# Layer 0 of a convolution and attention network: reciprocals of the softmax sums straight from PSUM, and the logits' bound on ScalarE and GpSimd

## The chip, the cores and the metric

The kernel runs on one core of a Trainium2 chip. The metric is the device time of one execution in microseconds (us). The core's engines work side by side, each through its own instructions in order: TensorE (PE in the profile, PEld for its weight loads), VectorE (DVE), ScalarE (ACT), GpSimd (POOL) and the queue of SyncE (SP), which issues the DMAs. SBUF is the memory that the engines work in, with 128 partitions; PSUM holds what TensorE writes.

## What is computed

Four layers follow each other on an input of 4 images of 128 channels and 64 x 64 pixels. Only layer 0 is concerned here. For one image, with q and v maps of 128 x 4096 and two maps w and b of 4096 values, it computes

```python
norm = jnp.sqrt(jnp.sum(q * q, axis=0))
k = q / jnp.clip(norm, 0.0001)[None, :]
logits = jnp.einsum('cn,cm->nm', k, q)
mean = jnp.mean(logits, axis=0, keepdims=True)
sparse = jax.nn.relu(logits - mean * w[None, :] + b[None, :])
mask = (sparse != 0.0).astype(logits.dtype)
attn = jax.nn.softmax(logits * sparse * SOFTMAX_SCALE, axis=0)
attn = jnp.clip(attn * mask, 1e-08)
out = jnp.einsum('cn,nm->cm', v, attn)
```

and then a 3 x 3 convolution of `out`, a leaky ReLU and the sum with the input. Here w and b come from small networks of q, with a leaky ReLU between two 1 x 1 convolutions.

## The kernel before

Layers 0 and 1 run one after the other for each image, with parts of layer 2 of the image before beside them; layer 3 comes last. Layer 0 is `layer0`. It cuts the 4096 columns m of an image into 8 chunks c of `NB` = 512, and the 4096 rows n into 16 pairs of 128. An item i is one chunk with one pair; there are 128 items in an image, and i = 16 c + m. In what follows "item m" is the place in the chunk. An item's tiles are 128 x 2 x 512.

The logits aren't divided by the softmax's sum before the product with v. `weights` computes max(logits + ncut, 0) x logits, where `ncut` is the negated threshold; `shifted` subtracts `bound`, an upper bound of the logits' products in a column, and takes the exponential; `sums` adds up the exponentials with TensorE, in four groups of 32 equal rows of one PSUM bank (`zs`). The clipping at 1e-8 of the quotient is a maximum with the sum times 1e-8 (`floored`, with `floor` in PSUM), and the division comes after the product with v, in `image`, as a factor `scale`. `masked` multiplies with the mask, on VectorE for even items and on GpSimd for odd ones, where ScalarE's Sign has made the mask first. `bound` is max(norm + ncut, 0) x norm for each column; the steps `top` and `top_b` of `thresholds` compute it.

The order of instructions is written out by hand and kept: `pinned` wraps the engines so that the program's order is each engine's order. The loop of `layer0` runs over the items. In item i VectorE does `weights` for i, `above` for i + 1 (logits + ncut) and `floored` for i - 18 (`LAG` is 18); TensorE does `logits` for i + 2, `product` for i - 19 and, every other item, `sums`; GpSimd does the subtraction of `shifted`, and every other item a masked product; ScalarE does the exponential, every other item a Sign, and in images 1 to 3 what `beside` calls: two exponentials over a row of layer 2 of the image before (`junk` in the profile), each with a read of its sum, and a load of `gp` every 16 items. The tile `t` has 21 buffers, so `above` waits for the product of an item 20 before it; the pairs of logits have two PSUM buffers, so `logits` waits for `weights` two items before it.

The small work of a chunk goes through `queue`, a list of runs of steps. In each item at most two steps that aren't marked `on_pe` are taken, until one that is marked comes up, and then that one. Where a run ends without a marked step, the first steps of the next run follow if there is room. These runs matter:

- `scales(c)`: its step `a` copies `zs` at item 0 of the next chunk; the others are put ahead of everything at item 1. `d` makes `floor` with a matmul and the sums as columns with four small ones (`zt_ps`); `f` takes the reciprocals of 128 x 4 (`rzt`); `g` spreads them to 128 x 512 with four matmuls (`rz_ps`); `h` copies this to `scale`.
- `thresholds(c + 1)`: put at the end of the queue at item 1. A load of `q` and `own` (the norms), four matmuls into `th_ps` with the steps `hidden`, `mean`, `times`, `cut` that use each, then `top` on GpSimd and `top_b` on VectorE.
- `convolved`: put at the end at item 3, just after `image`. Six steps with the nine taps, `leaky` on ScalarE, `add` on GpSimd with the store of x1.

The banks of PSUM are all in use: the pairs of logits have four, and `misc` (for `zt_ps`, `rz_ps`, `th_ps`, `conv_ps`, `v_ps`), `zs`, `fl` and `acc` one each. A step that takes a new `misc` tile waits until the old one has been read.

The lines L111 in the profile are those of a helper that records every pinned instruction, so groups are told apart by their tiles.

Of the kernel before, what the change touches and what calls it, by code (L numbers as in the profile page):

```python
# [8 lines left out]
F32 = mybir.dt.float32  # L9
BF16 = mybir.dt.bfloat16  # L10
AF = mybir.ActivationFunctionType
ALU = mybir.AluOpType
# [4 lines left out]
P = 128  # L17
IMG = 64
L = IMG * IMG
PADW = IMG + 2  # L20
NB = 512
# [8 lines left out]
class Queue:  # L30
# [21 lines left out]
    def on_pe(self):  # L52

        if not self.run and self.runs:
            self.run = self.runs.pop(0)
        return bool(self.run) and getattr(self.run[0], "pe", False)
# [59 lines left out]
class Net:  # L116
# [160 lines left out]
    def weights0(self):  # L277
        nc, pool = self.nc, self.later
        self.load_all(pool, ["lin_b"])
        self.load_rows(pool, ["lw2_b", "bw2_b"])  # L280

        M = self.ins["lw1_wT"].shape[1]
        self.w1_T = pool.tile([P, 2 * M], F32, name="w1_T", tag="w1_T")
        self.w1_b = pool.tile([2 * M, 1], F32, name="w1_b", tag="w1_b")
        self.w2 = pool.tile([2 * M, 2], F32, name="w2", tag="w2")
        nc.vector.memset(self.w2, 0.0)
        for i, n in enumerate(("lw", "bw")):
            r = slice(i * M, (i + 1) * M)
            nc.sync.dma_start(out=self.w1_T[:, r], in_=self.ins[f"{n}1_wT"])
            nc.sync.dma_start(out=self.w1_b[r, :], in_=self.ins[f"{n}1_b"])  # L290
            nc.sync.dma_start(out=self.w2[r, i : i + 1], in_=self.ins[f"{n}2_wT"])
        self.lw2_rep = self.replicated(pool, "lw2_rep", self.w2[:, 0:1])
        self.bw2_rep = self.replicated(pool, "bw2_rep", self.w2[:, 1:2])

        self.floor_c = pool.tile([P, P], F32, name="floor_c", tag="floor_c")
        nc.vector.memset(self.floor_c, 1e-8 / 32)
        self.quarter = pool.tile([P, 1], F32, name="quarter", tag="quarter")
        nc.vector.memset(self.quarter, 1.0 / 32)

    def weights12(self):  # L300
        nc, pool = self.nc, self.later
# [31 lines left out]
    def layer0(self, b):  # L333


        nc = self.nc
        pe, dve, act, pool, sp = self.pinned()
# [4 lines left out]
        with self.pool("l0", 1) as big, self.pool("l0t", 2) as tmp, self.pool("l0a", LAG + 3) as ap, \  # L342
# [6 lines left out]
            def misc(name, rows=P):  # L349
                return ps1.tile([rows, NB], F32, name=name, tag="misc")  # L350

            def row(name, bufs=2, rows=P):
                return tmp.tile([rows, NB], F32, name=name, tag=name, bufs=bufs)
# [8 lines left out]
            for c in range(0 if b else NCH):  # L362
                s = bass.ts(c, NB)
# [10 lines left out]
                own = row("own")  # L374
# [11 lines left out]
                for i in range(4):  # L386
                    nc.tensor.matmul(
                        inv_ps[:, bass.ts(i, P)], inv[:, i : i + 1].to_broadcast([P, P]), self.ident,
                        start=True, stop=True,
# [12 lines left out]
            held = {}  # L402
# [18 lines left out]
            qs, ncut, bound = {}, {}, {}  # L421

            def thresholds(c):


                s = bass.ts(c, NB)

                def load():
                    qs[c] = held["q"] = row("q")
                    sp.dma_start(out=qs[c], in_=self.q0[:, s])  # L430
                    held["own"] = row("own")
                    sp.dma_start(out=held["own"], in_=self.norms[:, s].to_broadcast([P, NB]))

                def into(rows, lhsT, key):
                    def go():
                        held["ps"] = misc("th_ps", rows)
                        pe.matmul(held["ps"], lhsT, held[key], start=True, stop=True)
                    return on_pe(go)

                def hidden():  # L440
                    held["h"] = row("h", 1, 64)
                    act.activation(held["h"], held["ps"], AF.Prelu, bias=self.w1_b, alpha=0.2)

                def mean():
                    held["m"] = row("m", 1)
                    act.copy(held["m"], held["ps"])

                def times():
                    dve.scalar_tensor_tensor(held["m"], held["ps"], self.lw2_b, held["m"], ALU.add, ALU.mult)

                def cut():
                    ncut[c] = row("ncut")
                    dve.scalar_tensor_tensor(ncut[c], held["ps"], self.bw2_b, held["m"], ALU.add, ALU.subtract)

                def top():
                    bound[c] = row("bound")
                    pool.tensor_tensor(bound[c], held["own"], ncut[c], ALU.add)

                def top_b():
                    dve.scalar_tensor_tensor(bound[c], bound[c], 0.0, held["own"], ALU.max, ALU.mult)  # L460

                return [
                    load, into(64, self.w1_T, "q"), hidden, into(P, kbar_rep, "q"), mean,
                    into(P, self.lw2_rep, "h"), times, into(P, self.bw2_rep, "h"), cut, top, top_b,
                ]

            def both(t):
# [2 lines left out]
            lg, t, e, zs, acc, floor, scale = {}, {}, {}, {}, {}, {}, {}  # L470
# [58 lines left out]
            def scales(c):  # L529

                def a():
                    held["z"] = row("z", 1)
                    act.copy(held["z"], zs.pop(c))

                def d():
                    floor[c] = ps1.tile([P, NB], F32, name="fl", tag="fl")
                    pe.matmul(floor[c], self.floor_c, held["z"], start=True, stop=True)
                    held["zt"] = misc("zt_ps")
                    for i in range(NB // P):
                        pe.matmul(  # L540
                            held["zt"][:, i : i + 1], held["z"][:, bass.ts(i, P)], self.quarter,
                            start=True, stop=True,
                        )

                def f():
                    held["rz"] = tmp.tile([P, NB // P], F32, name="rzt", tag="rzt")
                    dve.reciprocal(held["rz"], held["zt"][:, 0 : NB // P])

                def g():
                    held["zt"] = misc("rz_ps")  # L550
                    for i in range(NB // P):
                        pe.matmul(
                            held["zt"][:, bass.ts(i, P)], held["rz"][:, i : i + 1].to_broadcast([P, P]),
                            self.ident, start=True, stop=True,
                        )

                def h():
                    scale[c] = row("scale")
                    act.copy(scale[c], held["zt"])

                return [a, on_pe(d), f, on_pe(g), h]

            def image(c):
                dve.tensor_tensor(
                    ypad[:, 1 + c * ROWS : 1 + (c + 1) * ROWS, 1 : 1 + IMG],
                    acc.pop(c).rearrange("p (a b) -> p a b", b=IMG),
                    scale.pop(c).rearrange("p (a b) -> p a b", b=IMG), ALU.mult,
                )

            def convolved(c):  # L570
# [27 lines left out]

            beside = self.row_weights(b - 1, big, tmp) if b else lambda i: None
            queue.add(thresholds(0))  # L600
            if b:
                queue.step()
# [12 lines left out]
            for i in range(S + LAG + 2):  # L615
                c, m = divmod(i, U)
# [13 lines left out]
                if i in due:  # L630
                    d = due.pop(i)
                    image(d)
                    if d:
                        queue.add(convolved(d - 1))
                    if d == NCH - 1:
                        queue.add(convolved(d))
# [4 lines left out]
                if 0 < i <= S + 1:  # L641
                    if i <= S:
                        masked(i - 1)
                    if i % 2 == 0:
                        sums(i - 2)
                    if i % U == 0:
                        run = scales(i // U - 1)
                        run[0]()
                    elif i % U == 1 and i > U:
                        queue.first(run[1:])  # L650
                if i < S and m == 1 and c + 1 < NCH:
                    (queue.add if c else queue.first)(thresholds(c + 1))
# [1348 lines left out]
```

## Time and profile before

| what | value |
|---|---|
| median of three runs | 10654.12 us (10645.72 to 10660.42) |
| the profiled execution | 10664.21 us, of it a span of 10662.4 us from first to last instruction |
| mean granted TensorE clock | 0.896 |
| busy over the span: PE, DVE, ACT, POOL | 80%, 86%, 59%, 76% |
| `weights` of the first to the last item, image 0 | 65.1 to 689.1 us, 624.0 us |
| the same, image 1 | 1724.0 to 2362.4 us, 638.4 us |
| the same, image 2 | 3420.1 to 4057.8 us, 637.7 us |
| the same, image 3 | 5113.6 to 5751.9 us, 638.2 us |

Times are counted from the first instruction of the span. In a group of the profile the columns are line, engine, operation, tiles (written<-read), shapes and count, then busy time, the mean of one in ns, and the idle time just before it with what ended that. In a timeline they are start, duration (both us), engine, line, operation, tiles, shapes and count, with the idle time before it in square brackets. Durations of neighbours on one engine overlap by some 0.08 us, so a step's share of an engine is the distance between starts. The settled chunks of an image, 2 to 6, repeat themselves to within a few hundredths of a us, item by item.

### The profile page before, as it was taken

The numbers are of one execution on the slowest core, as the hardware profiler recorded it, in microseconds if no ns is written. First come the engines' busy times: TensorE is split into PE (matmuls) and PEld (weight loads), VectorE is DVE, ScalarE is ACT, GpSimd is POOL, SyncE is SP. The second block draws the span as 40 slices with busy tenths as digits, with TensorE's granted clock in tenths as the row PEclk, the third lists the DMA queues.
The fourth block names the chain that finished last, engine by engine and source line by source line (L and its number), as shares of the span: only waits on it lengthen the run. The fifth ranks groups of instructions, "written<-read, shape, count | busy, mean of one in ns | idle before, by whom it ended". The sixth has DMA issues, their size and how long they took to land. (4 is left out here: it accounts for less than half of the span.)

```text
span 10662.4 us, 91085 instructions
## 1 busy us (share of the span) xinstructions
PE 8514.6 (80%) x28080; PEld 3044.8 (29%) x28080; DVE 9216.5 (86%) x6390; ACT 6331.1 (59%) x9504; POOL 8117.2 (76%) x3542
## 2 busy tenths in 40 slices
PE   8996667997787997787898778877777777777775
PEld 3331212332223333223333222322222222222221
DVE  7869998886998885999886899449999999999996
ACT  3324445665665664666564666456666666666764
POOL 6748886765887774888674888339999999988986
PEclk9997778998998998999999899889898888888886
DMA  1008773006886003888100888248888888888886
GB/s 37 11 20 196 190 190 94 17 12 159 207 201 163 12 18 88 199 209 205 41 15 22 208 201 204 61 107 205 201 204 201 204 198 207 211 224 222 222 222 178
DMA packets 509431, 1543.30 MB, mean 145 GB/s; under 512 B 84208, under 2 KB 92016, under 8 KB 508944
## 3 DMA queue, kind: packets, MB, share of 16 engines
q1 hardware_dynamic: 508944, 1537.49, 58.1%
q8 instruction: 223, 3.65, 0.2%
q14 instruction: 264, 2.16, 0.1%
HBM read 1342.06 MB, written 132.24 MB: 138 GB/s over the span
## 5 line engine op out<-in xcount | busy, mean ns | idle before, releaser
L111 POOL TENSOR_TENSOR p<-h,c_rep 128x1024 f32<-128x1024 f32 x2048 | 4808.1, 2358 | 831.1 <-DVE h L111 769.9
L111 DVE TENSOR_TENSOR_SCAN h<-da,carry,db 128x1024 f32<-128x1024 f32 x1536 | 3603.6, 2346 | 198.0 <-ACT da L111 20.8
L111 PE MATMUL db<-parts,sel 96*128 96x512 bf16 x4096 | 1401.0, 428 | 1489.7 <-DVE h L111 1469.0
L111 DVE TENSOR_TENSOR db<-b_rep,db 128x1024 f32<-128x1024 f32 x1536 | 1854.5, 1207 | 195.7 <-DMA b_rep<-bc 128.6
L111 ACT ACTIVATE da<-row,A 128x1024 f32<-128x1024 f32 x1536 | 1761.0, 1147 | 321.5 <-DMA row<-d 318.2
L111 POOL TENSOR_TENSOR e<-e,bound 128x1024 f32<-128x1024 f32 x512 | 1240.7, 2425 | 572.6 <-DVE e L111 572.3
L111 POOL TENSOR_TENSOR x<-row,b_rep 128x1024 f32<-128x1024 f32 x512 | 1209.2, 2362 | 155.2 <-DMA row<-d 155.1
L111 PE MATMUL total<-p,gather 128*32 128x512 f32 x8192 | 1251.2, 730 | 10.4 <-POOL p L111 10.2
L111 DVE TENSOR_TENSOR_SCAN h<-db,carry,x 128x1024 f32<-128x1024 f32 x512 | 1194.8, 2334 | 72.5 <-ACT db L111 39.7
L111 ACT ACTIVATE db<-db,A 128x1024 f32<-128x1024 f32 x512 | 555.4, 1085 | 1149.9 <-PE db L111 1095.8
L111 PEld LDWEIGHTS <-sel 96*128 96x128 bf16 x4096 | 309.5, 101 | 3048.3 <-DVE h L111 2091.0
L111 ACT ACTIVATE e<-e 128x1024 f32<-128x1024 f32 x512 | 540.9, 1057 | 1054.3 <-POOL e L111 1054.3
L111 PE MATMUL lg<-q,k 128*128 128x512 f32 x2048 | 1022.8, 623 | 107.4 <-DVE e L111 99.0
L111 PE MATMUL acc<-t,vT 128*128 128x512 f32 x2048 | 956.1, 593 | 6.4 <-DVE t L111 3.3
L111 PE MATMUL acc<-e,values 128*128 128x512 f32 x1536 | 848.2, 643 | 92.0 <-ACT e L111 68.0
L111 DVE TENSOR_TENSOR t<-lg,ncut 128x1024 f32<-128x1024 f32 x512 | 624.6, 1220 | 286.0 <-PE acc L111 262.4
L111 ACT ACT_TABLE_LOAD x617 | 791.6, 1283 | 38.9 <-DMA r<-y 17.6
L111 ACT COPY carry<-h 128x1 f32<-128x1 f32 x2048 | 374.0, 185 | 487.5 <-DVE h L111 483.0
L111 ACT ACTIVATE e<-gq,below,fcol 128x512 f32<-128x512 f32 x768 | 610.1, 805 | 86.7 <-PE acc L111 86.5
L111 POOL TENSOR_TENSOR t<-t,e 128x1024 f32<-128x1024 f32 x256 | 609.9, 2383 | 45.4 <-ACT t L111 45.4
L111 ACT ACTIVATE junk<-gp,ntop,fcol 128x512 f32<-128x512 f32 x768 | 619.5, 807 | 26.8 <-DMA gp<-g 14.1
L111 DVE SCALAR_TENSOR_TENSOR e<-t,lg 128x1024 f32<-128x1024 f32 x512 | 618.9, 1209 | 1.2
(233 smaller groups left out, 9982.4 us busy)
## 6 DMA issues: line engine op xcount, KB each, us to landing
row<-d SPq DMA_DIRECT2D x2048, 512.0 KB
parts<-split SPq DMA_DIRECT2D x960, 64.0 KB
b_rep<-bc SPq DMA_DIRECT2D x96, 512.0 KB
c_rep<-bc SPq DMA_DIRECT2D x96, 512.0 KB
d<-delta SPq DMA_DIRECT2D x80, 384.0 KB
r<-y SPq DMA_DIRECT2D x48, 512.0 KB
xq<-in_x SPq DMA_DIRECT2D x72, 256.0 KB
res<-x SPq DMA_DIRECT2D x32, 512.0 KB
```

Of the source, the lines that this page charges most:

```text
L111: return self.tc.keep_in_program_order(method(*args, **kwargs))
```

## The change

Two parts, both in layer 0. In `scales` the four small matmuls for `zt_ps`, the reciprocals of 128 x 4, the four matmuls for `rz_ps` and the copy go. VectorE takes the reciprocal of `floor` in PSUM into `scale` in four pieces of 128 x 128, as four steps of the queue; `image` multiplies by 1e-8 as well, with another form of instruction. The constant `quarter` goes. In `thresholds`, `top_b` becomes a Relu on ScalarE, and a new step `top_c` multiplies by the norms on GpSimd.

```diff
-        self.quarter = pool.tile([P, 1], F32, name="quarter", tag="quarter")
-        nc.vector.memset(self.quarter, 1.0 / 32)
...
                 def top_b():
-                    dve.scalar_tensor_tensor(bound[c], bound[c], 0.0, held["own"], ALU.max, ALU.mult)
+                    act.activation(bound[c], bound[c], AF.Relu)
+
+                def top_c():
+                    pool.tensor_tensor(bound[c], bound[c], held["own"], ALU.mult)
...
                 def d():
                     floor[c] = ps1.tile([P, NB], F32, name="fl", tag="fl")
                     pe.matmul(floor[c], self.floor_c, held["z"], start=True, stop=True)
-                    held["zt"] = misc("zt_ps")
-                    for i in range(NB // P):
-                        pe.matmul(
-                            held["zt"][:, i : i + 1], held["z"][:, bass.ts(i, P)], self.quarter,
-                            start=True, stop=True,
-                        )
-
-                def f():
-                    held["rz"] = tmp.tile([P, NB // P], F32, name="rzt", tag="rzt")
-                    dve.reciprocal(held["rz"], held["zt"][:, 0 : NB // P])
-
-                def g():
-                    held["zt"] = misc("rz_ps")
-                    for i in range(NB // P):
-                        pe.matmul(
-                            held["zt"][:, bass.ts(i, P)], held["rz"][:, i : i + 1].to_broadcast([P, P]),
-                            self.ident, start=True, stop=True,
-                        )
-
-                def h():
-                    scale[c] = row("scale")
-                    act.copy(scale[c], held["zt"])
-
-                return [a, on_pe(d), f, on_pe(g), h]
+
+                def f(j):
+                    def go():
+                        if j == 0:
+                            scale[c] = row("scale")
+                        s = bass.ts(j, P)
+                        dve.reciprocal(scale[c][:, s], floor[c][:, s])
+                    return go
+
+                return [a, on_pe(d), *[f(j) for j in range(NB // P)]]
...
-                dve.tensor_tensor(
+                dve.scalar_tensor_tensor(
                     ypad[:, 1 + c * ROWS : 1 + (c + 1) * ROWS, 1 : 1 + IMG],
-                    acc.pop(c).rearrange("p (a b) -> p a b", b=IMG),
-                    scale.pop(c).rearrange("p (a b) -> p a b", b=IMG), ALU.mult,
+                    acc.pop(c).rearrange("p (a b) -> p a b", b=IMG), 1e-8,
+                    scale.pop(c).rearrange("p (a b) -> p a b", b=IMG), ALU.mult, ALU.mult,
                 )
```

## The prediction, as put on record

> **What bounds it now.** I read the slices of the page first (second view). They show four stretches with no DMA to speak of and TensorE at 9 tenths: layer 0 of the four images. The view of windows over those stretches comes next:
>
> ```profile
> 65.00:690.00 625.00, 590.77 (x1780) 231.23 (x1779) 549.93 (x473) 211.31 (x224) 465.87 (x202) 0.98 0.05 14
> 1724.00:2363.00 639.00, 589.15 (x1779) 230.18 (x1778) 558.20 (x469) 424.82 (x727) 465.27 (x202) 0.99 0.05 15
> ```
>
> Its columns are the stretch, its length, then busy time of PE, PEld, DVE, ACT and POOL, the granted clock, DMA. PE is busy 92 to 95%, DVE 87 to 88%, POOL 73%: no engine is the bound alone. ACT does twice as much in images 1 to 3 (424.8 against 211.3 us), because two `junk` pairs of `row_weights` follow each exponential there. The groups by line then give prices:
>
> ```profile
> L111 DVE SCALAR_TENSOR_TENSOR bound<-bound,own 128x512 f32<-128x512 f32 x32 | 75.6, 2364 | 6.1 <-POOL bound L111 6.1
> L111 DVE TENSOR_TENSOR t<-lg,ncut 128x1024 f32<-128x1024 f32 x512 | 624.6, 1220 | 286.0 <-PE acc L111 262.4 <-PE lg L111 23.5
> L111 POOL TENSOR_TENSOR e<-e,bound 128x1024 f32<-128x1024 f32 x512 | 1240.7, 2425 | 572.6 <-DVE e L111 572.3
> L111 DVE RECIPROCAL rzt<-zt_ps 128x4 f32<-128x4 f32 x32 | 5.5, 172 | 12.8 <-PE zt_ps L111 12.8
> ```
>
> DVE waits for PE (`above` for the product that frees its tile, 262 us), POOL for DVE (572 us). So place decides, not totals, and the timeline of one settled chunk (image 1, chunk 4) is the view that carries the rest. DVE at items 2 to 4:
>
> ```profile
> 2053.61 0.17 DVE L111 RECIPROCAL rzt<-zt_ps 128x4 f32<-128x4 f32 x1
> 2053.71 1.19 DVE L111 SCALAR_TENSOR_TENSOR e<-t,lg 128x1024 f32<-128x1024 f32 x1
> 2055.73 1.23 DVE L111 TENSOR_TENSOR t<-lg,ncut 128x1024 f32<-128x1024 f32 x1 [0.83 <-PE acc L111]
> ...
> 2061.25 1.23 DVE L111 TENSOR_TENSOR t<-lg,ncut 128x1024 f32<-128x1024 f32 x1 [0.30 <-PE acc L111]
> ...
> 2084.73 2.75 DVE L111 SCALAR_TENSOR_TENSOR bound<-bound,own 128x512 f32<-128x512 f32 x1
> ```
>
> An item begins at `e<-t,lg`. Item 2 runs from 2050.22 to 2053.71 (3.49 us) and is full of DVE work: no idle time is printed in it. PE in the same items:
>
> ```profile
> 2051.20 0.95 PE L111 MATMUL zt_ps<-quarter,z 128*128 128x1 f32 x8
> 2056.61 1.16 PE L111 MATMUL rz_ps<-ident,rzt 128*128 128x128 f32 x8
> 2061.88 1.07 PE L111 MATMUL th_ps<-q,w_T 128*64 128x512 f32 x2 [0.67 <-ACT scale L111]
> 2088.76 1.95 PE L111 MATMUL lg<-q,k 128*128 128x512 f32 x4 [0.83 <-DVE e L111]
> ```
>
> Up to the next start the two groups take 0.81 and 1.00 us, and PE waits 0.67 us for ScalarE's copy of `scale`.
>
> **What the Trainium skill says.** *SBUF — State Buffer*, section "SBUF: two separate sides": a VectorE operation with two SBUF inputs and a GpSimd operation exclude each other for a whole instruction. The trace agrees: `bound` takes 0.69 us at its shortest, and 2.75 when it comes 0.17 us after a GpSimd product. *VectorE: DVE Perf Modes*, "First, the fixed hardware budget": Reciprocal is an iterative divide with a repeat count of 8. The trace has no long one; see below. *ScalarE: Activation LUTs*, "Table sets: the hidden batching unit": relu is in every set. So no table load; no run here shows it, though Sign, Prelu and Exp alternate in this chunk without one. *TensorE: Matmul & The Clock Gate*, "Architectural detail": ScalarE's and VectorE's queues are strictly in order. It agrees: `y<-conv_ps` starts at 2118.04, when the junk pairs ahead of it are over.
>
> **Reciprocals, per chunk.** Removed: 16 small matmuls (1.81 us of PE), the 0.67 us wait, one 0.10 us DVE step, a 0.57 us copy on ScalarE. Added: four reciprocals of 128x128 from PSUM. After idle time one column takes 164 ns (`z`), four 183 (`rzt`, its longest), eight 203 (`split`): 5.6 ns a column. An estimate from this: 164 + 127 x 5.6 = 0.88 us, and as the next instruction starts some 0.08 us before an end, 0.80 us each. Bounds: one column a cycle (1.13 us / 1024 = 1.1 ns) gives 0.22; the page's eight cycles a column give 8 x 1.1 x 128 = 1.15 us. Eight columns at 203 speak against both ends. `image` becomes a form that costs 745 instead of 688 ns (as `ncut`, one PSUM input): +0.06. The scale is read some 16 items later, so it isn't late.
>
> Where it lands: the old queue ran d | f, g | h, and threshold steps. The new one runs d at item 1, two reciprocals at item 2, two at item 3, and no PE step follows there. DVE's item 2 has no slack: 3.49 becomes 3.39 + 1.60 = 4.99. Item 3 gets 1.60 + 0.06 and loses its 0.83 wait, since PE is now ahead. Item 4 loses 0.40 (3.79 to 3.39: the 0.30 and a slower start), item 5 about 0.5 of its 1.89 wait. So 3.20 + 0.06 - 0.10 is added, 0.83 + 0.40 + 0.50 comes back: **+1.4 us a chunk**. The PE time saved is in these recovered waits and nowhere else, because DVE ends last at items 2 and 3. With 0.22 us each it is about 0; with 1.15 it is +2.9.
>
> All later steps of the queue move one item on: the loads of `q` and `own` (still issued with the step ahead of the first threshold matmul; the 16 items hold the whole queue), the threshold matmuls, nine taps, `leaky`, `add`. SP's store of x1 moves with `add`, and the next `gp` load stands behind it; ScalarE waits up to 0.5 us a chunk for `gp` now, and I count nothing for it.
>
> **The bound, per chunk with a threshold behind it.** DVE loses its 2.75 us instruction. Items 8 and 9 took 6.55 + 4.74 = 11.29 us; items 12 and 13, with taps and without it, 3.92 + 6.29 = 10.21: -1.08. Added: a Relu of about 0.6 us (ACT's exponential of 1024 columns takes 1.06, half of it and its start) and a POOL product of 1.28 (as `bound<-own,ncut`). POOL's product waits for the Relu, and the Relu stands behind ACT's exponential of its item and the two junk pairs; behind the product in POOL's queue stands the next subtraction `e<-e,bound`. This is a wait that was not there:
>
> ```profile
> 2091.18 1.06 ACT L111 ACTIVATE e<-e 128x1024 f32<-128x1024 f32 x1 [3.74 <-POOL e L111]
> 2093.88 1.04 ACT L111 ACTIVATE t<-t 128x1024 f32<-128x1024 f32 x1
> 2093.43 2.37 POOL L111 TENSOR_TENSOR e<-e,bound 128x1024 f32<-128x1024 f32 x1 [2.29 <-DVE e L111]
> 2118.78 1.28 POOL L111 TENSOR_TENSOR y<-y,xq 128x512 f32<-128x512 f32 x1 [1.15 <-ACT y L111]
> 2122.41 1.06 ACT L111 ACTIVATE e<-e 128x1024 f32<-128x1024 f32 x1 [3.71 <-POOL e L111]
> ```
>
> Walked on with these durations: the Relu takes the place at 2093.88, POOL's product runs 2094.5 to 2095.8, the subtraction starts at 2095.8 in place of 2093.43, 2.4 late. POOL's masked product ends at 2100.5, DVE's masked product (ready at 2099.89) goes between, the next subtraction ends at 2104.0 (before 2100.44), its exponential and two junk pairs at 2106.8, Sign at 2107.8, the masked product that waits for Sign at 2110.2, the next subtraction at 2112.5; DVE's masked product, which ran at 2110.53, stands at the lock until then: 2.0 us lost on DVE. A precedent lies at item 15: `add`'s wait for `leaky` behind junk makes it 7.38 us, against 6.28 in image 0, 1.10 more. I take 2.5: 2.0 and some of a second such catch. Bounds: 0 (the lag is absorbed, POOL being busy 73%) and 4. Net +1.4 in images 1 to 3. In image 0 the Relu follows at once and delays POOL 0.6 us, which I take as hidden: -1.08.
>
> **The sum.** Images 1 to 3: 3 x (8 x 1.4 + 7 x 1.42) = 63.4. Image 0: 8 x 1.4 - 7 x 1.08 = 3.6. Together +67 us on the profiled span of 10662.4 (10664.2 with what lies around it), +0.63%; the profiled run is 10 above the median of 10654.1. On the median: **10722**. Only one memset in the start-up goes; layers 1 to 3 keep their instructions.
>
> **Rivals.** (1) *TensorE bounds layer 0, and its relief is the gain.* For it: 92 to 95% busy. Place: items 1 to 4; price: 2.48 us a chunk less 0.84 for four reciprocals of 0.22; it decides if these are that short and POOL's lag is absorbed. Then 32 x -1.64 - 28 x 1.08 = -83: 10571. Against it: eight columns at 203 ns, and DVE without slack at item 2. (2) *The lag is absorbed*, reciprocals as forecast: 32 x 1.4 - 28 x 1.08 = +15: 10669, no change. For it: POOL's 27% of idle time; against: item 15. (3) *Reciprocals at eight cycles a column*: 32 x 2.9 + 21 x 1.42 - 7.6 = +115: 10769. For it: the skill's repeat count; against: the eight-column row. That the change doesn't do what it says I leave out: the floor is the sum times 1e-8, and `image` multiplies by 1e-8.
>
> **How the numbers follow.** Forecast 0.62, rival 1 0.09, rival 2 0.12, rival 3 0.17. About 0.2% (21 us) is what a measurement can tell from no change. Faster 0.09, same 0.12, slower 0.79. The reciprocal's bounds shift the forecast by -45 to +48, the stall's by -53 to +32; taken together some -70 to +55. Cut at rival 2's side and at rival 3's: 10655 to 10775.
>
> **What would show it.** Right: reciprocals near 0.88 us; items 2 and 3 longer by 1.5 and 0.8; PE waits there for DVE's `e`; a new POOL wait for ACT's `bound` of 1 us or more in images 1 to 3, none to speak of in image 0; image 0 nearly unchanged, the others some 20 us longer. Wrong: reciprocals under 0.5 us, or layer 0 shorter in all images with DVE still waiting for PE at items 2 to 5; or the time outside layer 0 changing.

## The result, and the profile after

| what | before | after |
|---|---|---|
| median of six runs each | 10652.09 us (10645.72 to 10660.42) | 10719.32 us (10711.84 to 10733.21) |
| ratio after / before, 95% interval | | 1.0064 [1.0051, 1.0077] |
| the profiled execution, its span | 10664.21, 10662.4 us | 10718.85, 10717.1 us |
| layer 0, image 0 (first to last `weights`) | 624.0 us | 629.3 us |
| layer 0, images 1, 2, 3 | 638.4, 637.7, 638.2 us | 655.2, 655.2, 655.3 us |

The kernel became 67 us slower by the medians and 54.6 by the two profiled executions, since the one of before lay 12 us above its median. Layer 0 grew by 56.7 us; the stretches before, between and after changed by -2 us in total. So in this pair the whole loss is in layer 0: +5.3 us in image 0, +17 in each of the others.

The view of windows of the changed kernel, over layer 0 of images 0 and 1 (columns as before: stretch, length, busy PE, PEld, DVE, ACT, POOL, clock, DMA):

```profile
65.00:694.00 629.00, 575.95 (x1666) 216.80 (x1664) 570.55 (x486) 211.37 (x223) 471.66 (x208) 0.99 0.05 14
1731.00:2386.00 655.00, 587.30 (x1665) 219.83 (x1664) 585.30 (x482) 422.81 (x726) 486.92 (x208) 0.97 0.05 15
```

PE has some 114 matmuls less and is busy 90 to 92% instead of 92 to 95%; what it was relieved of did not shorten the stage. DVE went from 558.2 to 585.3 us in image 1. The groups by line of the changed kernel say with what:

```profile
L111 DVE TENSOR_TENSOR t<-lg,ncut 128x1024 f32<-128x1024 f32 x512 | 624.2, 1219 | 232.8 <-PE acc L111 201.8 <-PE lg L111 29.1
L111 POOL TENSOR_TENSOR t<-t,e 128x1024 f32<-128x1024 f32 x256 | 607.1, 2372 | 120.2 <-ACT t L111 120.2
L111 DVE SCALAR_TENSOR_TENSOR t<-t,e 128x1024 f32<-128x1024 f32 x256 | 520.0, 2031 | 26.3 <-ACT e L111 25.7
L111 DVE RECIPROCAL scale<-fl 128x128 f32<-128x128 f32 x128 | 112.0, 918 | 8.8 <-PE fl L111 8.8
L111 POOL TENSOR_TENSOR bound<-bound,own 128x512 f32<-128x512 f32 x32 | 41.8, 1306 | 78.0 <-ACT bound L111 74.7 <-DVE t L111 3.3
```

Of these, the two masked products have to be set beside the same groups of the kernel before, which were not shown yet:

```profile
L111 POOL TENSOR_TENSOR t<-t,e 128x1024 f32<-128x1024 f32 x256 | 609.9, 2383 | 45.4 <-ACT t L111 45.4
L111 DVE SCALAR_TENSOR_TENSOR t<-t,e 128x1024 f32<-128x1024 f32 x256 | 428.0, 1672 | 18.8 <-ACT e L111 18.5
```

Four readings. The reciprocals cost 112 us in all. DVE's idle time before `above` fell from 286 to 233 us (its wait for PE's product from 262 to 202), so part of this is taken from idle time. DVE's masked product is the same instruction on the same data, and yet its mean rose from 1672 to 2031 ns, 92 us in all. That is waiting, which the profile counts as busy: this instruction reads two tiles in SBUF, and it and a GpSimd instruction exclude each other, as the prediction cites. Below this exclusion is called the lock. And POOL has two new idle times: 74.7 us for ACT's Relu (`bound`) and 75 more for ACT's Sign (120.2 against 45.4).

DVE at items 2 to 4 of the chunk that the prediction used (image 1, chunk 4), timeline of the changed kernel:

```profile
2065.31 1.21 DVE L111 SCALAR_TENSOR_TENSOR e<-t,lg 128x1024 f32<-128x1024 f32 x1
...
2069.42 1.76 DVE L111 RECIPROCAL scale<-fl 128x128 f32<-128x128 f32 x2
2071.10 1.16 DVE L111 SCALAR_TENSOR_TENSOR e<-t,lg 128x1024 f32<-128x1024 f32 x1
...
2075.04 2.19 DVE L111 SCALAR_TENSOR_TENSOR t<-t,e 128x1024 f32<-128x1024 f32 x1
2077.15 1.75 DVE L111 RECIPROCAL scale<-fl 128x128 f32<-128x128 f32 x2
2078.83 1.16 DVE L111 SCALAR_TENSOR_TENSOR e<-t,lg 128x1024 f32<-128x1024 f32 x1
```

Item 2 is now 5.79 us (2065.31 to 2071.10), item 3 7.73. That is +2.30 and +1.71, more than the reciprocals alone bring (+1.58 and +0.73, run e1 below). The rest is a wait of 0.63 us for `floor` in item 2, whose matmul waits for a late copy of the sums on ScalarE, and in item 3 the masked product, which takes 2.19 us here and 1.22 before and in e1. TensorE stands behind it, in its own timeline there:

```profile
2075.27 1.96 PE L111 MATMUL acc<-t,vT 128*128 128x512 f32 x4 [0.68 <-DVE ypad L111]
2080.04 3.43 PE L111 MATMUL lg<-q,k 128*128 128x512 f32 x4 [2.82 <-DVE e L111]
```

Before, DVE waited there for PE (0.83 us, shown in the prediction); now PE waits 2.82 us for DVE's `e`. The other part lies at items 10 to 13, where the Relu is. ACT in the timeline:

```profile
2109.09 1.06 ACT L111 ACTIVATE e<-e 128x1024 f32<-128x1024 f32 x1 [3.09 <-POOL e L111]
2110.06 0.80 ACT L111 ACTIVATE junk<-gp,ntop,fcol 128x512 f32<-128x512 f32 x1
...
2110.98 0.81 ACT L111 ACTIVATE junk<-gp,ntop,fcol 128x512 f32<-128x512 f32 x1
...
2111.80 0.62 ACT L111 ACTIVATE bound<-bound 128x512 f32<-128x512 f32 x1
```

and POOL in the same items:

```profile
2112.49 1.28 POOL L111 TENSOR_TENSOR bound<-bound,own 128x512 f32<-128x512 f32 x1 [3.42 <-ACT bound L111]
2113.72 2.37 POOL L111 TENSOR_TENSOR e<-e,bound 128x1024 f32<-128x1024 f32 x1
...
2125.57 2.39 POOL L111 TENSOR_TENSOR t<-t,e 128x1024 f32<-128x1024 f32 x1 [1.52 <-ACT t L111]
2127.91 2.35 POOL L111 TENSOR_TENSOR e<-e,bound 128x1024 f32<-128x1024 f32 x1
```

and DVE's masked product at item 13, in the kernel before and in the changed one:

```profile
2110.53 1.22 DVE L111 SCALAR_TENSOR_TENSOR t<-t,e 128x1024 f32<-128x1024 f32 x1
...
2127.97 3.37 DVE L111 SCALAR_TENSOR_TENSOR t<-t,e 128x1024 f32<-128x1024 f32 x1
```

It reads as the prediction walked it: the Relu behind the exponential and two junk pairs, POOL idle for 3.42 us, its queue late, then a second wait of 1.52 us for Sign, and at the end DVE's masked product, which starts 0.06 us after POOL's subtraction (2127.91), waits out the whole of it and takes 3.37 us instead of the 1.22 that it needs when nothing is in its way.

To see what a chunk gained and lost, I added up, from the trace, what the masked products took over 1.22 us each ("lock"), VectorE's idle time, nearly all of it for `acc`, and its own instruction on `bound`. Each is the mean of chunks 3 to 6, called a settled chunk below. (Chunk 2, which the text ahead of the prediction counts among the settled ones, takes 79.2 us in images 1 to 3 before, not 82.5.) All in us:

| kernel, images | chunk | lock | DVE idle | DVE on `bound` |
|---|---|---|---|---|
| before, image 0 | 80.38 | 1.70 | 10.01 | 2.23 |
| before, images 1 to 3 | 82.49 | 2.62 | 10.75 | 2.75 |
| after, image 0 | 81.09 | 4.37 | 7.16 | 0 |
| after, images 1 to 3 | 84.59 | 6.82 | 8.23 | 0 |

In images 1 to 3, four reciprocals at a spacing of 0.84 add 3.36, `rzt` goes (-0.10), `bound` goes (-2.67 as a spacing), the lock adds 4.20, and 2.52 of idle time is used up: +2.27, where the chunk grew by 2.10. In image 0 it is 3.36 - 0.10 - 2.16 + 2.67 - 2.85 = +0.92, for +0.71.

### The profile page after: what moved, and what is told of

The parts are those of the page before. It is cut to its first block, busy times and chain, and to the rows that moved or that the text cites. A ratio compares the mean times of both kernels' runs of the same rounds, so it can differ in the third digit from the quotient of the medians.

```text
span 10717.1 us, 90072 instructions
## 1 busy us (share of the span) xinstructions
PE 8472.2 (79%) x27489; PEld 2995.5 (28%) x27568; DVE 9331.6 (87%) x6453; ACT 6325.4 (59%) x9504; POOL 8197.7 (76%) x3574
## 5 line engine op out<-in xcount | busy, mean ns | idle before, releaser
L111 POOL TENSOR_TENSOR e<-e,bound 128x1024 f32<-128x1024 f32 x512 | 1282.0, 2510 | 414.9 <-DVE e L111 398.0
L111 POOL TENSOR_TENSOR t<-t,e 128x1024 f32<-128x1024 f32 x256 | 607.1, 2372 | 120.2 <-ACT t L111 120.2
L111 ACT ACTIVATE e<-gq,below,fcol 128x512 f32<-128x512 f32 x768 | 610.1, 805 | 82.7 <-PE acc L111 82.6
L111 DVE TENSOR_TENSOR t<-t,fl 128x1024 f32<-128x1024 f32 x512 | 614.8, 1210 | 7.3 <-PE fl L111 7.1
```

The lines of the kernel that those rows point to most:

```text
L111: return self.tc.keep_in_program_order(method(*args, **kwargs))
```

## The experiments

Theory 1 is the prediction's: two separate losses, reciprocals at items 2 and 3 where DVE has no slack, and POOL's wait for a Relu behind the junk pairs. Rival A: the Relu's chain is hidden. Rival B: POOL's 1.28 us of extra work through the lock is the cost, not the wait. Rival C: DVE's 3.3 us count wherever they are put. Rival D: the one-item shift of the queue is the cost, not the reciprocals' time. All results first; each ratio is against the kernel before on the same chip, and an image of layer 0 runs from its first to its last `weights`. The runs were made on several chips, so between them the ratios are the better comparison.

| run | median, us | ratio, 95% interval | images 0, 1, 2, 3, us |
|---|---|---|---|
| before | | | 624.0 638.4 637.7 638.2 |
| after | 10719.32 | 1.0064 [1.0051, 1.0077] | 629.3 655.2 655.2 655.3 |
| e1_recip_only | 10702.11 | 1.0041 [1.0026, 1.0056] | 631.8 649.2 647.6 647.5 |
| e2_bound_only | 10671.48 | 1.0011 [1.0005, 1.0018] | 618.1 644.1 646.5 642.3 |
| e3_gap | 10746.78 | 1.0080 [1.0065, 1.0096] | 645.0 654.7 655.4 653.7 |
| e4_spread | 10712.94 | 1.0050 [1.0033, 1.0067] | 621.5 658.1 655.7 659.7 |
| e5_relu_ahead | 10699.83 | 1.0044 [1.0028, 1.0060] | 632.2 649.2 645.4 647.4 |
| e6_one_column | 10663.95 | 1.0010 [1.0003, 1.0017] | 612.2 647.0 649.2 648.9 |
| e7_pool_max | 10684.65 | 1.0023 [1.0013, 1.0033] | 619.8 652.4 653.3 652.4 |
| e8_product_next | 10698.13 | 1.0040 [1.0027, 1.0053] | 632.0 647.8 648.4 647.7 |
| e9_spread_dve | 10661.40 | 1.0005 [0.9997, 1.0014] | 623.7 646.6 644.8 645.6 |
| e10_bound_ahead | 10636.30 | 0.9986 [0.9979, 0.9992] | 618.0 633.6 635.0 634.0 |
| e11_spread_ahead | 10661.69 | 1.0004 [0.9996, 1.0012] | 621.4 648.2 642.7 647.6 |

An image repeats itself within a few us only: its first chunks differ from run to run. Small effects are read from the settled chunks, which are steadier, but not everywhere: in images 1 to 3 of e1, e5 and e8 chunk 3 is still 1.7 to 1.9 us shorter than chunks 4 to 6, and in those of e2, e3, e6, e7 and e11 the four chunks lie 1.7 to 4.6 us apart. Outside layer 0, where no edit changes more than a memset, the profiled executions differ from that of before by -19 us (e7) to +17 us (e3), and why is not known. So the images show what happens in layer 0, and only the ratios, from many executions, what a kernel is worth.

### The reciprocals alone

```diff
-                    act.activation(bound[c], bound[c], AF.Relu)
-
-                def top_c():
-                    pool.tensor_tensor(bound[c], bound[c], held["own"], ALU.mult)
+                    dve.scalar_tensor_tensor(bound[c], bound[c], 0.0, held["own"], ALU.max, ALU.mult)
...
```

> The reciprocals from PSUM alone; the bound stays on VectorE as before. Theory 1 (two separate losses, the reciprocals' at items 2 and 3 and GpSimd's wait for the Relu in images 1 to 3): +1.4 us a chunk in every image, images 11 us longer each, +45 us in all (10697), items 2 to 5 as in the changed kernel. Rival A (the reciprocals are the whole loss, the Relu's chain is hidden): all of the +67 us, images 1 to 3 as long as in the changed kernel (655 us from the first to the last item).

Measured: +43 us by the medians, +38 in layer 0. Items 2 and 3 of image 1, chunk 4 take 5.07 + 6.75 us, against 3.49 + 6.02: +2.3. A settled chunk of images 1 to 3 grew by 1.18 (83.67), of image 0 by 1.30. But one number was not expected. The view of the tile `bound`, in the kernel before and in this run (min/median/max in ns, then first and last start):

```profile
L111 DVE SCALAR_TENSOR_TENSOR bound<-bound,own x32: 685/2748/2841, 62.7 to 5639.3; 128x512 f32<-128x512 f32 x32
L111 DVE SCALAR_TENSOR_TENSOR bound<-bound,own x32: 676/679/2840, 61.5 to 5687.3; 128x512 f32<-128x512 f32 x32
```

One item later in the queue, this instruction mostly no longer meets a POOL product at the lock. The reciprocals' part so carries a gain of some 2 us a chunk that belongs to the shift, and the masked products take much of it back: the lock in images 1 to 3 rose from 2.62 to 3.86, in image 0 from 1.70 to 3.55.

### The bound alone

```diff
-                    dve.scalar_tensor_tensor(bound[c], bound[c], 0.0, held["own"], ALU.max, ALU.mult)
+                    act.activation(bound[c], bound[c], AF.Relu)
+
+                def top_c():
+                    pool.tensor_tensor(bound[c], bound[c], held["own"], ALU.mult)
...
```

(against the kernel before)

> The bound by Relu and GpSimd's product alone; the sums' reciprocals as before. Theory 1: image 0 about 8 us shorter (VectorE's 2.75 us instruction gone), images 1 to 3 about 10 us longer each (2.5 us of stall against 1.08 saved, seven times), +22 us in all (10674), with 1 us or more of GpSimd wait for the Relu a chunk in images 1 to 3. Rival A: all images 8 us shorter, -30 us in all (10622).

Measured: image 0 5.9 us shorter, images 1 to 3 together 18.6 longer. Both signs of the forecast are there (-7.6 and +29.8), at a smaller size. Rival A falls: a hidden chain would have shortened all four images. This part and the one before add up to +55 us, the whole change gives +67; with intervals of plus or minus 7 to 16 us on each the difference is at the edge of what can be told, but e5 below names a reason for it.

### Is it the wait? A step's distance between Relu and product

First an empty step between the two, which takes a place in the queue of small steps:

```diff
-                    into(P, self.lw2_rep, "h"), times, into(P, self.bw2_rep, "h"), cut, top, top_b, top_c,
+                    into(P, self.lw2_rep, "h"), times, into(P, self.bw2_rep, "h"), cut, top, top_b, end, top_c,
```

> The changed kernel with an empty step between the Relu and the product, so that GpSimd's product comes one item after the Relu and the taps one item later. Theory 1: GpSimd no longer waits for the Relu, the stall of 2.5 us goes in images 1 to 3: 17 us shorter each than in the changed kernel, 10667 in all; image 0 unchanged. Rival A, and rival B (not the wait but GpSimd's 1.28 us of extra work is what costs): no more than 5 us gained in all, 10715.

Measured: nothing gained in images 1 to 3, and image 0 15.7 us longer. By the forecasts this is rival A's and B's result, and worse. But the empty step moves the nine taps behind it too, and chunks 4 to 6 of image 0 went from 81.2 to 84.7 us with it, while they stay at 81.2 in the next run, where the taps keep their place. So this run doesn't decide. The product was moved by itself, to the next item, with the taps where they were (`soon`, a list, is emptied once an item, ahead of the queue):

```diff
+                def top_b_then():
+                    top_b()
+                    soon.append(top_c)
...
-                    into(P, self.lw2_rep, "h"), times, into(P, self.bw2_rep, "h"), cut, top, top_b, top_c,
+                    into(P, self.lw2_rep, "h"), times, into(P, self.bw2_rep, "h"), cut, top, top_b_then if c else top_b, end if c else top_c,
...
+                while soon:
+                    soon.pop()()
```

> The changed kernel with GpSimd's product one item after the Relu and nothing else moved: the taps stay where the changed kernel has them (in the run with the gap they moved too). Theory 1: no wait for the Relu, images 1 to 3 some 17 us shorter than the changed kernel's 655 each, image 0 unchanged at 629. Rival B: the wait goes and the time stays, images 1 to 3 within 5 us of 655.

Measured: 21 us less than the whole change by the medians, 26 by the ratios; images 1 to 3 are 7 us shorter each, where Theory 1 said 17 and rival B less than 5. The groups by line of this run:

```profile
L111 POOL TENSOR_TENSOR t<-t,e 128x1024 f32<-128x1024 f32 x256 | 607.9, 2375 | 43.4 <-ACT t L111 43.3
L111 POOL TENSOR_TENSOR bound<-bound,own 128x512 f32<-128x512 f32 x32 | 41.0, 1281 | 3.0 <-ACT bound L111 3.0
```

The same product at nearly the same mean (1281 ns, 1306 in the whole change), without the wait: POOL's idle time for Sign is back at 43 us (45 before), and 3 are left for the Relu. So the wait counts, and the second one, for Sign, comes from it. Rival B falls as the only cause; POOL's 1.28 us remain in this run.

### The Relu ahead of the junk pairs

```diff
+                def top_a():
+                    top()
+                    if c:
+                        early.append(top_b)
...
-                    into(P, self.lw2_rep, "h"), times, into(P, self.bw2_rep, "h"), cut, top, top_b, top_c,
+                    into(P, self.lw2_rep, "h"), times, into(P, self.bw2_rep, "h"), cut, top_a, end if c else top_b, top_c,
...
+                while early:
+                    early.pop()()
                 beside(i)
```

> The changed kernel with the Relu issued on ScalarE ahead of the item's two junk pairs, the product in the same item as before, taps where they are. Theory 1 (GpSimd's wait for a Relu that stands behind the junk pairs is the cost in images 1 to 3): the wait falls from 2.7 us to under 1 us a chunk, images 1 to 3 are some 10 us shorter each than the changed kernel's 655, 10690 in all. Rival B (the product's 1.28 us of GpSimd time, which pushes the next subtraction into VectorE's masked product at the lock, is the cost): images 1 to 3 stay above 650 us.

Measured: 10699.8, again 20 us less than the whole change; in images 1 to 3 a settled chunk takes 83.08 instead of 84.59 and POOL's wait for the Relu is 1.69 instead of 3.43 us a chunk, not under 1 as expected. So the place behind the junk pairs cost 1.5 us a settled chunk (1.1 if the three images are divided by their 21 chunks). What is left is the second finding: with the wait halved this kernel is still no faster than the one with the reciprocals alone (1.0044 against 1.0041), though a settled chunk is 0.59 us shorter. The instruction that the Relu spares DVE took 2.75 us in most chunks of the old queue, and 0.68 once the queue had shifted.

### Reciprocals of one column

`same` is one tile, set to ones at the start of the layer. The kernel leaves out all but four columns of the scale.

```diff
...
-                        if j == 0:
-                            scale[c] = row("scale")
-                        s = bass.ts(j, P)
-                        dve.reciprocal(scale[c][:, s], floor[c][:, s])
+                        s = slice(j * P, j * P + 1)
+                        scale[c] = same
+                        dve.reciprocal(same[:, s], floor[c][:, s])
```

> The changed kernel with reciprocals of one column each in place of 128, into a row that is otherwise all ones: most of the scale is left out, so the output isn't the reference's, and VectorE's cost of the reciprocals falls from 3.3 to about 0.4 us a chunk. Theory 1: item 2 falls to 3.6 us and item 3 to 5.1, TensorE's relief of 1.81 us counts in part: 2 to 3 us a chunk better than the changed kernel, image 0 at 610 us, 10640 in all. Rival D (the shift of the queue by one item, not the reciprocals' time, is what costs): less than 1 us a chunk, 10695 or more.

Measured: image 0 17.1 us shorter than with the whole change, the others 6 to 8 each; 10664 in all, where Theory 1 said 10640 and rival D 10695 or more. The view of the tile `same` in this run:

```profile
L111 DVE RECIPROCAL same<-fl x128: 140/148/168, 148.5 to 5779.4; 128x1 f32<-128x1 f32 x128
```

The 0.75 us less in each of the four is 3 us of DVE a chunk. Image 0 gets 2.1 a chunk of it, images 1 to 3 0.9: there the lock (7.34 in place of 6.82) and the idle time (9.60 in place of 8.23) take most of it back. The run bears on what TensorE's relief is worth, too. It differs from the bound alone (e2) in having no sums by matmul, nearly no reciprocals and the shifted queue, and relief and shift can't be told apart in it: image 0 is 5.9 us shorter, 0.7 us a chunk of the 2.48 removed, and images 1 to 3 are together 12 us longer. Rival D falls for image 0. In images 1 to 3 it stays open: even with reciprocals that cost next to nothing they are 9 to 12 us longer than before, but POOL's wait for the Relu (3.43 us a chunk) is in them too.

### Reciprocals one by one at items 9 to 12

```diff
-                        queue.first(run[1:])
+                        queue.first(run[1:2])
+                        pieces = run[2:]
+                if i > U and 9 <= m <= 12 and pieces:
+                    pieces.pop(0)()
```

> The changed kernel with the four reciprocals taken one by one at items 9 to 12, where TensorE has taps and VectorE was idle 0.9 to 1.7 us an item; threshold and tap steps come two items earlier than in the changed kernel. Theory 1: the reciprocals go into VectorE's idle time, the 1.5 and 0.8 us at items 2 and 3 go and TensorE's relief starts to count: some 2 us a chunk better than the changed kernel, 10655 in all; the GpSimd stall stays. Rival C (VectorE's 3.3 us of added work costs wherever it is put): no change from the changed kernel, 10719.

Measured: image 0 8 us shorter, the others no shorter (655.7 to 659.7); 10713 in all, near rival C's 10719 and far from Theory 1's 10655. The thresholds and taps come two items earlier here; in images 1 to 3 the wait for Sign rises to 4.56 us a settled chunk, the lock to 7.95. So the same with `bound` on DVE as before, which has no Relu to wait for:

```diff
                 def top_b():
-                    act.activation(bound[c], bound[c], AF.Relu)
-
-                def top_c():
-                    pool.tensor_tensor(bound[c], bound[c], held["own"], ALU.mult)
+                    dve.scalar_tensor_tensor(bound[c], bound[c], 0.0, held["own"], ALU.max, ALU.mult)
...
```

> The reciprocals from PSUM taken one by one at items 9 to 12, and the bound on VectorE as before: the two remedies together. Theory 1: image 0 at 622 us or less as in the run with spread reciprocals and the changed bound, images 1 to 3 without the GpSimd stall at some 632 us: about 20 us under the kernel before, 10635. Rival C (in images 1 to 3 the spread reciprocals cost 1 us a chunk whatever the bound): images 1 to 3 at 645 or more, no gain over the kernel before.

Measured: 1.0005 [0.9997, 1.0014]. A settled chunk takes 82.70 us in images 1 to 3 against 82.49 before, and 79.57 in image 0 against 80.38. By the forecasts on record this is rival C's result: images 1 to 3 at 645 or so and no gain over the kernel before. Against C speaks e1, which has the same work with the reciprocals at items 2 and 3: there a settled chunk takes 83.67 and 81.68 us, so the later place is worth 1.0 us in images 1 to 3 and 2.1 in image 0 (thresholds and taps moved with it). The 3.3 us of new DVE work are not free, though: the kernel comes out even because DVE's `bound` takes 0.68 us in place of 2.75 here too and 3.6 us of idle time are used up, while the lock rises from 2.62 to 5.31. So place counts, but rival C isn't ruled out for images 1 to 3. What remains of the images' +7 us lies mostly in the first chunks, where chunk 1 of image 1 takes 86.5 us instead of 81.9; I didn't find out why.

### Max and product on GpSimd

The spread of e4 (its edit isn't repeated), with `top_b` as a maximum with zero on GpSimd:

```diff
-                    act.activation(bound[c], bound[c], AF.Relu)
+                    pool.tensor_scalar(bound[c], bound[c], 0.0, None, ALU.max)
...
```

> Reciprocals one by one at items 9 to 12, and the bound with no ScalarE in it: maximum and product are two GpSimd instructions in a row. No round trip between engines is left, but GpSimd works some 0.7 to 1.3 us more a chunk. Theory 1 (the round trip costs): as the run with the Relu ahead, or a few us better. Rival B (GpSimd's time at the lock costs): 5 to 20 us worse than the run with the Relu ahead.

Measured: 10684.7, 28 us less than e4: POOL's wait for the Relu is gone, that for Sign stays at 4.56 us a settled chunk. It isn't cheap either; its tile `bound`, then one case from the timelines of POOL and DVE:

```profile
L111 POOL TENSOR_SCALAR bound<-bound x32: 1488/2458/2480, 59.5 to 5670.1; 128x512 f32<-128x512 f32 x32
...
2078.19 2.11 DVE L111 SCALAR_TENSOR_TENSOR t<-t,e 128x1024 f32<-128x1024 f32 x1
2079.18 2.46 POOL L111 TENSOR_SCALAR bound<-bound 128x512 f32<-128x512 f32 x1
```

About 1 us of the 2.46 is the lock: in 28 of the 32 the maximum starts some 1 us after a masked product of DVE and runs beside it, and in the four where no masked product runs it takes 1.49. The run is 20 us above e11 by the ratios (1.0023 against 1.0004), which is the forecast of rival B: GpSimd's own time counts as well as the wait, here with 2.46 us in place of the 0.7 to 1.3 expected.

### What beats both

The bound's part alone, with the Relu ahead of the junk pairs (the edits of e2 and of e5 on the kernel before, whose sums stay):

```diff
...
-                    into(P, self.lw2_rep, "h"), times, into(P, self.bw2_rep, "h"), cut, top, top_b,
+                    into(P, self.lw2_rep, "h"), times, into(P, self.bw2_rep, "h"), cut, top_a, end if c else top_b, top_c,
...
+                while early:
+                    early.pop()()
                 beside(i)
```

> The kernel before with the bound by Relu and GpSimd alone, the Relu issued ahead of the junk pairs; the sums' reciprocals stay as before. If the reciprocals' +1.4 us a chunk and the Relu's place are the two losses, neither is left and the saving of VectorE's bound shows in every image: image 0 at 618 us as with the bound alone, images 1 to 3 at 632 instead of 638, some 25 us under the kernel before (ratio 0.998). If GpSimd's product costs by itself through the lock with VectorE's masked products (rival B), images 1 to 3 stay at 638 or more and the ratio is 1.000.

Measured: 0.9986 [0.9979, 0.9992], some 15 us faster than the kernel before and 83 faster than the changed one. ACT in its timeline:

```profile
2071.10 1.06 ACT L111 ACTIVATE e<-e 128x1024 f32<-128x1024 f32 x1 [2.12 <-POOL e L111]
2072.06 0.61 ACT L111 ACTIVATE bound<-bound 128x512 f32<-128x512 f32 x1
2072.58 0.80 ACT L111 ACTIVATE junk<-gp,ntop,fcol 128x512 f32<-128x512 f32 x1
```

and POOL:

```profile
2071.02 2.38 POOL L111 TENSOR_TENSOR t<-t,e 128x1024 f32<-128x1024 f32 x1
2073.37 1.27 POOL L111 TENSOR_TENSOR bound<-bound,own 128x512 f32<-128x512 f32 x1
```

The Relu is over at 2072.67, while POOL is still busy with its masked product: no wait is printed. A settled chunk of images 1 to 3 takes 81.41 us, 1.08 less than before. GpSimd's product isn't free here either: the lock is 4.86 us a settled chunk in place of 2.62. Against e2, which differs in nothing but the Relu's place, the ratio falls from 1.0011 to 0.9986: this is the cleanest proof of the wait. The whole change with both remedies, the edits of e4 and of e5 together, gives no change that can be told:

> The whole change with both remedies: reciprocals one by one at items 9 to 12, Relu ahead of the junk pairs. Without a remedy it is 67 us over the kernel before, with the first alone 54, with the second alone 46. If the two losses are separate, both are gone: image 0 at 621, images 1 to 3 at 637 to 640, no more than 5 us from the kernel before. If what is lost is time at the lock between VectorE and GpSimd, which either of the two additions fills, 20 us or more stay (ratio 1.002 or more).

Measured: 1.0004 [0.9996, 1.0012], settled chunks 79.33 us in image 0 and 82.44 in the others, with a long chunk 1 in images 1 and 3 (86.1, but 82.6 in image 2). By the ratio the total is as forecast (+4 us); images 1 to 3, at 643 to 648 us, are not (637 to 640).

## Why the prediction was right, point by point

The time was right (+67 forecast, +67 by the medians), and so were its two causes and, in the main, its places. That it came out to the microsecond is luck: the two profiled executions give +54.6, images 1 to 3 grew by 17 us each where 21 was forecast, and terms that were wrong cancelled.

- **The reciprocal's size: right.** 887 to 959 ns, mean 918, at spacings of 0.81 to 0.87; forecast 0.88 and 0.80. This was worked out from rows of one, four and eight columns, and rival 3, with eight cycles a column (1.15 us), falls with it. The eight cycles were the prediction's own reading: the skill's page gives a repeat count of 8 and no time for a column. Rival 3's +2.9 us a chunk also left out the overlap of 0.08 that the forecast took off; with it the sum is +2.5.
- **Items 2 and 3: right for the reciprocals alone, too small for the whole change.** +2.31 us in e1 against +2.33; item 4 -0.46 against -0.40. Item 5 lost 0.58 in image 1 as forecast, but gained 0.15 in image 0. In the changed kernel items 2 and 3 of the same chunk grew by 4.01. With the Relu's wait shortened or gone (e5, e8) they are 5.07 and 6.75 us again, as in e1, so the lag behind the Relu reaches into these items of the next chunk, where the forecast had no part of it. PE waits for `e` there, as said. The reciprocals' part measured +43 us against +45. Its working was less complete than its sum: that the queue's shift takes `bound` out of the lock (2.75 to 0.68 us) and that masked products wait 1.2 to 1.9 us more were both left out.
- **`image` +0.06: wrong, and without weight.** 685 ns against 688.
- **-1.08 for the bound: right in the old queue, wrong in the new one.** e10 has -1.08 a settled chunk in images 1 to 3, though not where it was booked: 0.65 of it at items 8 and 9, 0.41 at item 12; in image 0 it has -0.80. But the forecast added it to a queue that its own first part had moved; after the shift a settled chunk saves 0.59 (e5 against e1), and the medians show nothing of it (-2 us).
- **The stall: mechanism right, size wrong.** The walk's waits for Relu and for Sign, and the catch at the lock, are in the trace. The term was 2.5 us a chunk; e5 and the whole change differ by 1.1 to 1.5, e10 and e2 by 1.4 to 1.7. The wait of POOL itself is larger than the 2.4 us of the walk (3.43), but part of the lag is absorbed, as rival 2 had it for all of it. Of a saving of some 30 us half or less came, and the stall was some 20 to 30 us too large. These two errors leave the part at +24 by the ratios of e1 and of the whole change, where +22 was forecast.
- **Image 0 "nearly unchanged": right in size (+5.3, forecast +3.6), by another sum.** No wait to speak of was forecast, but POOL waits 1.69 us a chunk for the Relu. The masked products lose 2.67 more at the lock, 1.85 of it in e1 too, where there is no Relu, and 2.85 of idle time is used up.
- **Rival 1, TensorE as the bound: fell.** It asked for reciprocals of 0.22 us, and they took 0.92. With reciprocals of 148 ns the kernel is still not faster than before (e6, 1.0010), and in image 0 e6 gains 0.7 us a chunk on e2, where this rival had 1.64. The shifted queue and the Relu's wait are in these figures too, so TensorE's relief alone is not measured.

Not settled: why chunk 1 grows by 4 to 5 us in most images where the reciprocals are spread (e9, e11), why the taps one item later cost 3.5 us a chunk in image 0 (e3), and how much of the reciprocals' part in images 1 to 3 is the shift of the queue (rival D) or stays wherever they are put (rival C).

## What to carry to other kernels

Where two engines exclude each other over SBUF, an edit that moves a hand-ordered queue by one step changes who meets whom: price each part in the queue that the other part leaves, not in the old one, and look at the mean of unchanged instructions for the waiting that is counted as busy. Work moved to an engine with room is only free if its place in that engine's queue lets it finish before the consumer is idle: here one Relu behind two independent exponentials turned a gain of 0.14% into a loss of 0.11%. Work that replaces many small matmuls is better placed at the items where its engine waits than where the data first come up: here that was worth 1.0 to 2.1 us a settled chunk (e9 against e1), though not enough for a gain over the kernel before.

## What the runs showed of the hardware

- VectorE's reciprocal from PSUM takes 148 ns for one column (e6) and 895 for 128 (the changed kernel; both medians): 5.9 ns a column, far above the elementwise rows of the same engine (1.19 us for 1024 columns).
- GpSimd's maximum with a constant over 128 x 512 took 1.49 us where no masked product of VectorE ran beside it, more than its product of two tiles of that size (1277 ns in the same run, e7); beside one it took 2.45 to 2.48.
- The lock over SBUF between VectorE and GpSimd: an instruction of 1.22 us took 3.37 when GpSimd came 0.06 us earlier. The Trainium skill, *SBUF — State Buffer*, section "SBUF: two separate sides", says that whichever starts first has it for the whole instruction; this trace agrees, and shows what the change added to this waiting: 92 us of VectorE's time over the kernel.
- The Relu ran beside Sign and Exp in 0.62 us, and no load of a table stands in layer 0 of the changed kernel's trace, from the first to the last `weights` of any image.
